# Banded attention in a decoder layer: where the value blocks are fetched, when the scores start, and when the first expert tile comes

## The chip, the cores and the metric

One core of one Trainium2 chip. The metric is the device time of one execution in microseconds (us); lower is better. All data are float32.

## The reference

A decoder layer with normalisation after each part, on 8 batches of 512 rows of 256 channels. There are three parts, and each adds its output to its input and normalises the rows:

```python
x = layernorm(x + banded_attention(x))        # 16 heads of 16 channels, window of 17 rows
x = layernorm(x + cross_attention(x, ctx))    # causal, one head of 256 channels, keys = values = ctx
x = layernorm(x + experts(x))                 # top 2 of 8 experts, 256 -> 1024 -> 256, gelu
```

The first part has a soft window, whose width and sharpness come out of each row:

```python
q = ln(silu(x @ Wq)); k, v = split(silu(x @ Wkv)); k = ln(k)      # ln by head
wp = silu(x @ Wwin + bwin)
width, sharp = sigmoid(wp[..., :16]) * 8 + 0.5, sigmoid(wp[..., 16:]) * 9.5 + 0.5
scores[l, h, w] = sum_d q[l, h, d] * k[l + w - 8, h, d] / 4        # w = 0..16
mask = sigmoid((width - abs(w - 8)) * sharp)
attn = softmax(scores - (1 - mask) * 10000)
out = silu((sum_w attn[w] * v[l + w - 8]) @ Wout)
```

The third part picks two experts a row by `x @ router_w.T`, weighs them by a softmax over the two, and adds `gelu(x @ w1[e].T) @ w2[e].T` of each.

## The kernel before

Five engines run instruction streams of their own: PE (matrix products and transposes), DVE (vector work), ACT (activations and copies), POOL (here nearly all DMA issues, the indirect ones among them) and SP (DMA issues alone). A scheduler decides the order on all but SP; SP's stream has the order in which the kernel's text is traced. `issue_after(ins)` puts the next instruction behind `ins` on the same engine.

The work is a software pipeline over rounds b = -2 to 8. A round lets several streams run side by side: cross-attention and routing of batch b (`crossed`), the weighted sums of banded attention of batch b+1 (`attended`), projections and scores of batch b+2 (`scores`), loads (`fetched`), and the expert tiles that can be run by then (`experts`). `together` (L1114) takes steps from the streams by their shares of the round: each stream has an amount of work, a start and an end in the round, and the stream with the least progress steps next. That sets the order in which the text is traced, SP's order, and the scheduler's preference.

Banded attention of a batch:

- `scores` projects the rows (L321, L322), normalises q and k, transposes them (L367), and multiplies q against k for half of the heads at a time (c = 0, 1) into `row`, which ACT's queue stores to a scratch in DRAM (`band`). `read_scores(c)` (L384) reads the band back in the layout of the softmax, `s`, by a DMA on POOL. `ws` (L395, POOL) carries what the mask is made of, `pen`. The values are stored to `vband`, and for batches 0 to 2 (`BANDED` = 3) two blocks of them, `vblock`, 320 KB each, are read back at L443 by POOL. In this kernel that happens a round before they are used, between and after the two score reads.
- `summed` (L497, batches 0 to 2) takes the softmax of each half on DVE and ACT, beginning with L519 (`s` and `pen`) and ending with L534 (times 1/sum). SP stores the weights to DRAM, `aband` (L541; c = 0 in four pieces, c = 1 in one), and fetches them back in blocks of 128 rows, `arow`, 160 KB each as two DMAs (`fetch`, L503, L507), of which two fit. There are eight blocks (two halves by four groups g0 to g3). PE transposes each (`paT`, L579), DVE and ACT copy the result (`aT`, L583), and PE multiplies it with `vblock` (`pw`, L557). Batches 3 to 7 go through `weighted`, which has neither.
- `attended` multiplies the sums with Wout (`py`, L599), ACT applies silu into `y` (L607, one buffer), DVE adds it to the rows (L609, twice a batch), and `layernorm` follows: statistics and `off` (L292) on DVE, the rows themselves on ACT (L295).

Cross-attention transposes the context and the rows (L248), multiplies (L715) and takes its softmax (with the transposes `pt` of L704 behind it). `route` picks the experts, copies a token's number into the rows (L811, an entry of the list `urgent`), and scatters the rows to the experts' regions in DRAM, `sorted_x` (L819, POOL); `plan` (L834) lays out the tiles that are ready, and its last DVE instruction (L903) is an entry of `urgent` too.

An expert tile is loaded by `load_tile` on SP (L937): two numbers read from memory (L940, L941), two halves of w1 (L961) and of w2 (L967), 512 KB each, and the rows `xs` (L946). The first tile of a round waits for the scatters before it, and has its `xs` behind the weights. `turned` transposes `xs` on PE (`pxs`, L1001). Round b = 1 has the first tile of all, one.

Of the kernel before, what the change touches and what calls it, by code (L numbers as in the profile page):

```python
# [10 lines left out]
ALU = mybir.AluOpType  # L11
# [4 lines left out]
L = 512  # L16
# [6 lines left out]
C = HH * D  # L23
QB = P // 2
SPAN = QB + W - 1
# [19 lines left out]
def decoder_layer_kernel(  # L45
# [16 lines left out]
    nc = tc.nc  # L62
    B = x.shape[0]
# [105 lines left out]
    def blank_rows(at):  # L169
# [2 lines left out]
            sorted_x[bass.ds(at, TS), :].rearrange("(p f) c -> p (f c)", p=P), blank  # L172
        )

    scattered, adds, out_of, read, turns, urgent = [], [], {}, [], [], []

    vband = [
        [dpool.tile([L + 2 * HALO, C], F32, name=f"vband{u}{c}") for c in range(2)]  # L180
        for u in range(2)
    ]
# [122 lines left out]
    def scores(b, xb):  # L305
# [129 lines left out]
        vh = []  # L435
        if b < BANDED:
            vb = apool.tile([P, 2, L // QB, C], F32, tag="vh", name="vblock", bufs=2)
        for c in range(2):
            src = vband[b % 2][c][:, :]
            if b < BANDED:  # L440

                with tc.issue_after(read[-1].ins):
                    nc.gpsimd.dma_start(  # L443
                        vb[0:SPAN, c],
                        bass.AP(
                            tensor=src.tensor,
                            offset=src.offset,
                            ap=[[C, SPAN], [QB * C, L // QB], [1, C]],
                        ),
                    )  # L450
                vh.append(vb[:, c])
                yield 0.3
                if c == 0:
                    read_scores(1)
                continue
            vhc = apool.tile([P, T + 2 * HALO, C], F32, tag="vh", name="vhalo", bufs=2)
            with tc.issue_after(read[-1].ins):
                nc.gpsimd.dma_start(
                    vhc.rearrange("p t c -> p (t c)"),
                    bass.AP(  # L460
                        tensor=src.tensor,
                        offset=src.offset,
                        ap=[[T * C, P], [1, (T + 2 * HALO) * C]],
                    ),
                )
            vh.append(vhc)
            yield 0.3
            if c == 0:
                read_scores(1)
# [27 lines left out]
    def summed(b):  # L497


        groups = [(c, g) for c in range(2) for g in range(T)]  # L500
        rows_of = {}

        def fetch(c, g):  # L503
            ar = apool.tile([P, HG, SPAN, 2], F32, tag="a", name="arow", bufs=2)
            for u in range(2):
                ub = (g * P + u * QB) * (LINE + 2)
                nc.sync.dma_start(  # L507
                    ar[u * QB : (u + 1) * QB].rearrange("p r k u -> p (r k u)"),
                    aband[c][ub : ub + QB * LINE].rearrange("(p n) -> p n", p=QB),
                )  # L510
            rows_of[c, g] = ar

        s, pen, vh = out_of.pop(b)
        for c in range(2):
            sc = s[c]


            with tc.issue_after(urgent[-1].ins) if urgent and c == 0 else nullcontext():
                nc.vector.scalar_tensor_tensor(  # L519
                    sc, pen[:, c], -4.0e4, sc, ALU.mult, ALU.add  # L520
                )
            flat = sc.rearrange("p t r w u -> p (t r) w u")
            byw = sc.rearrange("p t r w u -> p (t r) u w")
            full = [P, T * HG, W, 2]
            top = spool.tile([P, T * HG, 2], F32, tag="top", name="top")
            nc.vector.tensor_reduce(top, byw, AX.X, ALU.max)
            nc.vector.tensor_tensor(
                flat, flat, top[:, :, None, :].to_broadcast(full), ALU.subtract
            )
            nc.scalar.activation(sc, sc, AF.Exp, scale=0.25)  # L530
            den = spool.tile([P, T * HG, 2], F32, tag="den", name="den")
            nc.vector.tensor_reduce(den, byw, AX.X, ALU.add)
            nc.vector.reciprocal(den, den)
            nc.vector.tensor_tensor(  # L534
                flat, flat, den[:, :, None, :].to_broadcast(full), ALU.mult
            )
            lines = aband[c].rearrange("(p t n) -> p t n", p=P, t=T)[:, :, 0:LINE]

            parts = T if c == 0 else 1
            for ps in (slice(k * P // parts, (k + 1) * P // parts) for k in range(parts)):  # L540
                nc.sync.dma_start(  # L541
                    lines[ps].rearrange("p t (r n) -> p t r n", r=HG)[:, :, :, 0 : 2 * W],
                    sc[ps].rearrange("p t r w u -> p t r (w u)"),
                )
            if c == 0:

                for early in groups[:2]:
                    fetch(*early)
            yield 5.0
        oT = apool.tile([P, KC, L], F32, tag="T", name="oT", bufs=4)  # L550
        aT = apool.tile([P, 2, HG, 2, P], F32, tag="prod", name="aT")

        def sums(c, g):
            po = ps_o.tile([P, 2, 2, QB], F32, tag="o", name="pw")
            for u in range(2):
                for r in range(HG):
                    nc.tensor.matmul(  # L557
                        po[32 * r : 32 * r + 32, u],
                        vh[c][0:SPAN, 2 * g + u, 32 * r : 32 * r + 32],
                        aT[0:SPAN, g % 2, r, :, u * QB : (u + 1) * QB],  # L560
                        start=True,
                        stop=True,
                    )

            to = oT[:, c, g * P : (g + 1) * P].rearrange("c (u q) -> c u q", u=2)
            nc.scalar.mul(to, po[:, :, 0, :], par[:, 0:1])
            nc.vector.scalar_tensor_tensor(
                to, po[:, :, 1, :], par[:, 1:2], to, ALU.mult, ALU.add
            )

        for k, (c, g) in enumerate(groups):
            if 2 <= k + 1 < len(groups):
                fetch(*groups[k + 1])
            ar = rows_of.pop((c, g))
            for i in range(2):
                pt = ps_h.tile([P, 2, 2, P], F32, tag="h", name="paT")
                for r in range(2):
                    for u in range(2):
                        nc.tensor.transpose(  # L579
                            pt[0:SPAN, r, u, :], ar[:, 2 * i + r, :, u], ident  # L580
                        )
                put = nc.scalar.copy if i else nc.vector.tensor_copy
                put(aT[0:SPAN, g % 2, 2 * i : 2 * i + 2], pt[0:SPAN])  # L583
            if k:
                sums(*groups[k - 1])
            yield 1.4
        sums(*groups[-1])
        yield 0.8
        return oT

    def attended(b, xb):

        oT = yield from (summed if b < BANDED else weighted)(b)
        for jj in range(T // 2):
            py = ps_m.tile([P, 2, E], F32, tag="m", name="py")
            for j in range(2):
                for kc in range(KC):
                    at = (2 * jj + j) * P
                    nc.tensor.matmul(  # L599
                        py[:, j, :],  # L600
                        oT[:, kc, at : at + P],
                        wout_sb[:, kc, :],
                        start=(kc == 0),
                        stop=(kc == KC - 1),
                    )
            y = spool.tile([P, 2, E], F32, tag="y", name="y", bufs=1)
            nc.scalar.activation(y, py, AF.Silu)  # L607
            xj = xb[:, 2 * jj : 2 * jj + 2, :]
            nc.vector.tensor_tensor(xj, xj, y, ALU.add)  # L609
            yield 2.4  # L610
        layernorm(xb)
        yield 2.6
# [522 lines left out]
    had = 0  # L1135
    for b in range(-2, B + 1):
        streams = [(fetched(b), 1.0, 0.45, 1.0)] if b > -2 else []
        if 0 <= b < B:
            streams.append((crossed(b), 31.0, 0.0, 0.93))
        if 0 <= b + 1 < B:  # L1140
            streams.append((attended(b + 1, rows[b + 1][:, :, 0:E]), 29.4 if b + 1 < BANDED else 60.0, 0.08, 1.0))
        if b + 2 < B:
            streams.append((scores(b + 2, rows[b + 2][:, :, 0:E]), 38.0, 0.0, 0.88))
        m = max(0, -((NX * (TS - 1) - 2 * L * b) // TS)) if b < B else tiles_max
        if m > had:
            streams.append((experts(m - had, b == B), (m - had) * 7.2, 0.0, 1.0))
            had = m
        together(*streams)

# [56 lines left out]
```

## Time and profile before

| | |
| --- | --- |
| time, median of 3 runs | 1030.87 us (1028.61 to 1030.87) |
| profiled execution, its own time | 1036.22 us |
| its span (first to last instruction) | 1034.5 us |
| mean granted PE clock | 0.929 |
| PE, DVE, ACT, POOL busy | 903.6, 639.8, 549.1, 253.6 us |
| DMA moved | 252.09 MB, mean 244 GB/s |
| `vblock` fetches | 6 on POOL, 1.08 us each to issue, 5.3 to 7.7 us to landing |
| `arow` fetches on SP | 48 DMAs of two halves, 160.0 KB each |

A page describes one execution. Busy times count instructions that work, not the issue of DMAs, branches or waits. A line of the waits names an engine and a line of the kernel, what it waited for, the us in all, how often, and the longest. A line of the timeline has the start in us, the duration, the engine (a `q` behind it: its DMA issues), line, operation, tiles as out<-in, and in brackets the idle time before it and what ended that.

### The profile page before, as it was taken

How to read it: one execution, taken by the hardware profiler on the slowest of the kernel's cores; microseconds unless marked ns; L12 is line 12 of the kernel's file. 1: busy time of each engine (PE TensorE's matmuls, PEld its weight loads, DVE VectorE, ACT ScalarE, POOL GpSimd, SP SyncE). 2: the span in 40 equal slices, each digit the busy share in tenths (PEclk: the TensorE clock that was granted, in tenths of full speed). 3: DMA queues.
4: the chain of work that ended last, by engine and by line, in shares of the span. 5: the costliest groups of instructions: out<-in, count | busy, mean ns of one | idle time of the engine just before them, and what ended most of it. 6: DMA issues, size and time to landing. Idle time of an engine off the chain costs nothing. (4 is left out here: it accounts for less than half of the span.)

```text
span 1034.5 us, 18962 instructions
## 1 busy us (share of the span) xinstructions
PE 903.6 (87%) x6336; PEld 753.2 (73%) x6336; DVE 639.8 (62%) x2130; ACT 549.1 (53%) x955; POOL 253.6 (25%) x211
## 2 busy tenths in 40 slices
PE   5758888679989899999999989999999988999970
PEld 3435565457678778787788678888998988999960
DVE  5375773773689879979994989399943331111106
ACT  4465655567556647677755775476365311222224
POOL 1101000400411241125222522252341241121221
PEclk9588897889889899999999999899999999999995
DMA  8585654673798879588879897998898899999949
GB/s 207 145 139 142 128 129 113 194 160 89 254 343 252 250 273 298 174 263 308 264 218 273 293 282 195 273 343 290 258 282 256 274 266 379 319 331 318 335 114 323
DMA packets 129267, 252.09 MB, mean 244 GB/s; under 512 B 29680, under 2 KB 76848, under 8 KB 127888
## 3 DMA queue, kind: packets, MB, share of 16 engines
q1 hardware_dynamic: 89456, 183.30, 55.2%
q0 software_dynamic: 17824, 41.86, 16.4%
q10 hardware_dynamic: 21888, 25.70, 9.3%
q8 instruction: 52, 0.85, 0.3%
q14 instruction: 47, 0.39, 0.1%
HBM read 193.44 MB, written 57.36 MB: 242 GB/s over the span
## 5 line engine op out<-in xcount | busy, mean ns | idle before, releaser
L1015 PEld LDWEIGHTS ph<-xsT,w1h 128*128 128x128 f32 x2176 | 263.8, 195 | 14.0 <-DVE xsT L1004 4.9
L1015 PE MATMUL ph<-xsT,w1h 128*128 128x128 f32 x2176 | 270.5, 280 | 3.1 <-DVE xsT L1004 3.0
L1032 PE MATMUL pf<-w2h,h 128*128 128x256 f32 x1088 | 256.7, 387 | 3.3 <-ACT h L1023 3.3
L1032 PEld LDWEIGHTS pf<-w2h,h 128*128 128x128 f32 x1088 | 204.3, 194 | 32.6 <-ACT h L1023 5.7
L1041 POOL DMA_INDIRECT total<-ye,toi x68 | 122.3, 1798 | 420.5 <-ACT ye L1040 121.7
L1023 ACT ACTIVATE h<-ph 128x512 f32<-128x512 f32 x136 | 81.2, 598 | 121.7 <-PE ph L1015 116.7
L1004 DVE COPY xsT<-pxs 128x256 f32<-128x256 f32 x68 | 28.5, 419 | 175.2 <-PE pxs L1001 175.2
L655 DVE TENSOR_TENSOR prod<-prod 128x1024 f32<-128x1024 f32 (+3 forms) x160 | 103.3, 645 | 0.3
L1040 ACT ACTIVATE ye<-pf,g 128x256 f32<-128x256 f32 x68 | 32.2, 473 | 125.0 <-PE pf L1032 115.5
L647 DVE TENSOR_TENSOR prod<-vhalo,a 128x2176 f32<-128x2176 f32 x40 | 96.4, 2410 | 0.2
L819 POOL DMA_INDIRECT sorted_x<-xr,to x64 | 78.4, 1225 | 23.4 <-issue 16.4
L413 PE MATMUL pq<-kT,qT 32*64 32x160 f32 x1024 | 60.1, 389 | 17.5 <-DVE row L422 9.4
L387 POOL DMA_DIRECT2D s<-band x16 | 24.3, 1520 | 205.6 <-DMA band<-row 98.3
L321 PE MATMUL pa<-wall,xT 128*128 128x512 f32 x128 | 69.3, 629 | 5.5 <-ACT qk L323 2.8
L413 PEld LDWEIGHTS pq<-kT,qT 32*64 32x64 f32 x1024 | 36.0, 156 | 33.3 <-DVE row L422 11.9
L1023 ACT ACT_TABLE_LOAD x39 | 50.0, 1283 | 7.2 <-PE ph L1015 5.7
L422 ACT COPY row<-pq 128x320 f32<-128x320 f32 x104 | 37.9, 433 | 29.8 <-PE pq L413 24.7
L322 PEld LDWEIGHTS pb<-wall,xT 128*128 128x128 f32 x128 | 24.9, 197 | 35.8 <-issue 24.7
L579 PE MATMUL paT<-ident,arow 128*80 128x128 f32 x192 | 32.0, 309 | 18.3 <-DMA arow<-aband 14.0
L322 PE MATMUL pb<-wall,xT 128*128 128x288 f32 x128 | 42.4, 419 | 4.1 <-DVE wp L325 2.5
L689 PE MATMUL po<-c,prT 128*128 128x256 f32 x160 | 40.9, 386 | 4.3 <-ACT prT L708 4.2
L295 ACT ACTIVATE xr<-xr,off,rs 128x256 f32<-128x256 f32 x64 | 33.2, 592 | 21.2 <-DVE off L292 21.1
(196 smaller groups left out, 1376.7 us busy)
## 6 DMA issues: line engine op xcount, KB each, us to landing
w1h<-in_w_dram SPq DMA_DIRECT2D x136, 512.0 KB
w2h<-in_w_dram SPq DMA_DIRECT2D x136, 512.0 KB
band<-row ACTq DMA_DIRECT2D x64, 320.0 KB
vhalo<-vband POOLq DMA_DIRECT2D x10, 1280.0 KB, 9.6
xs<-sorted_x SPq DMA_DIRECT2D x68, 132.5 KB
arow<-aband SPq DMA_DIRECT2D x48, 160.0 KB
s<-band POOLq DMA_DIRECT2D x16, 272.0 KB, 6.3
xr<-in_x_dram SPq DMA_DIRECT2D x8, 512.0 KB
```

The costliest lines, as they stand in the source:

```text
L321: nc.tensor.matmul(pa, lhs, wall[:, kc, 0 : 2 * E], **se)
L322: turns.append(nc.tensor.matmul(pb, lhs, wall[:, kc, 2 * E :], **se))
L413: nc.tensor.matmul(pq[r][u * QB : (u + 1) * QB, ii], qT[rs, c, at : at + QB], kT[rs, c, :, at : at + SPAN].rearrange("p u k -> p k u"), st ...
L422: put(row[:, :, r], pq[r])
L647: nc.vector.tensor_tensor(prod.rearrange("p w (h d) -> p w h d", d=D), vh[c][:, t : t + W, :].rearrange("p w (h d) -> p w h d", d=D), a[:, ...
L655: nc.vector.tensor_tensor(prod[:, 0:n, :], prod[:, 0:n, :], prod[:, n : 2 * n, :], ALU.add)
L689: nc.tensor.matmul(po, probsT[j][:, i * P : (i + 1) * P], c[:, i, :], start=(i == 0), stop=(i == j),)
L819: sent = nc.gpsimd.indirect_dma_start(out=sorted_x[:, :], out_offset=bass.IndirectOffsetOnAxis(ap=to[:, n, j : j + 1], axis=0), in_=xr[:, ...
L1015: nc.tensor.matmul(ph[:, u, :], w1s[hf][:, kc, f * P : (f + 1) * P], xT[:, kc, :], start=(kc == 0), stop=(kc == KC - 1),)
L1023: nc.scalar.activation(h, ph, AF.Gelu)
L1032: nc.tensor.matmul(po, hs[fc // HU][:, fc % HU, j * P : (j + 1) * P], w2s[hf][:, f, :], start=(fc == 0), stop=(fc == NF - 1),)
L1041: add = nc.gpsimd.indirect_dma_start(out=total[:, :], out_offset=bass.IndirectOffsetOnAxis(ap=toi[:, j : j + 1], axis=0), in_=y, in_offset ...
```

## The change

There are three edits. The `vblock` fetches leave `scores` and POOL; SP issues them in `summed`, for each half after the store of that half's weights, and ahead of the fetches of `arow` that come next. The list `added` keeps the additions of `y` to the rows, and the first instruction of the c = 0 softmax of a batch is put behind the last entry of `urgent`, or, while that is empty, of `added`. When it is traced for batch 1, `urgent` is empty. The stream of experts starts at 0.45 of its round, not at 0, where no tile has been run before, which is in round b = 1 alone.

By the text and the streams, SP's order in round 1 goes from `where`, w1, w2, `xs`, then stores and fetches of batch 2's weights, to: stores of c = 0, `vblock`, fetches of g0 and g1, store of c = 1, `vblock`, fetch of g2, loads of x and of the context, `where`, w1, w2, `xs`, fetch of g3 and the others.

```diff
-    scattered, adds, out_of, read, turns, urgent = [], [], {}, [], [], []
+    scattered, adds, out_of, read, turns, urgent, added = [], [], {}, [], [], [], []
...
             if b < BANDED:
 
-                with tc.issue_after(read[-1].ins):
-                    nc.gpsimd.dma_start(
-                        vb[0:SPAN, c],
-                        bass.AP(
-                            tensor=src.tensor,
-                            offset=src.offset,
-                            ap=[[C, SPAN], [QB * C, L // QB], [1, C]],
-                        ),
-                    )
                 vh.append(vb[:, c])
                 yield 0.3
                 if c == 0:
...
-            with tc.issue_after(urgent[-1].ins) if urgent and c == 0 else nullcontext():
+            first = (urgent or added)[-1:] if c == 0 else []
+            with tc.issue_after(first[0].ins) if first else nullcontext():
                 nc.vector.scalar_tensor_tensor(
                     sc, pen[:, c], -4.0e4, sc, ALU.mult, ALU.add
                 )
...
                     sc[ps].rearrange("p t r w u -> p t r (w u)"),
                 )
+
+            src = vband[b % 2][c][:, :]
+            nc.sync.dma_start(
+                vh[c][0:SPAN],
+                bass.AP(
+                    tensor=src.tensor,
+                    offset=src.offset,
+                    ap=[[C, SPAN], [QB * C, L // QB], [1, C]],
+                ),
+            )
             if c == 0:
 
                 for early in groups[:2]:
...
-            nc.vector.tensor_tensor(xj, xj, y, ALU.add)
+            added.append(nc.vector.tensor_tensor(xj, xj, y, ALU.add))
...
-            streams.append((experts(m - had, b == B), (m - had) * 7.2, 0.0, 1.0))
+
+            begin = 0.0 if had else 0.45
+            streams.append((experts(m - had, b == B), (m - had) * 7.2, begin, 1.0))
             had = m
```

## Prediction

> **What bounds the kernel now.** I read the page first, for the busy shares and the 40 slices. The page's first part has PE at 87% of the span with no other engine near it. The second part shows where PE isn't full: up to the tenth slice (25.9 us each, so up to about 260 us), at the ninth, and at the end.
>
> ```profile
> span 1034.5 us, 18962 instructions
> PE 903.6 (87%) x6336; PEld 753.2 (73%) x6336; DVE 639.8 (62%) x2130; ACT 549.1 (53%) x955; POOL 253.6 (25%) x211
> PE   5758888679989899999999989999999988999970
> ```
>
> Then the window table, cut at the rounds that the diff touches (round A: batch 0's weighted sums; B: batch 1's; C: batch 2's, halved at 208), and the rest. Columns: window, its length, busy us of PE, PEld, DVE, ACT and POOL, granted PE clock, DMA share, GB/s.
>
> ```profile
> 44.00:103.00 59.00, 41.91 (x410) 28.10 (x409) 33.48 (x66) 33.10 (x59) 6.98 (x7) 0.79 0.70 149
> 103.00:178.00 75.00, 61.96 (x478) 42.70 (x476) 48.03 (x141) 46.69 (x88) 5.33 (x6) 0.86 0.57 121
> 178.00:208.00 30.00, 20.26 (x69) 13.26 (x69) 19.64 (x86) 15.60 (x26) 11.53 (x11) 0.84 0.64 194
> 208.00:266.00 58.00, 51.72 (x456) 38.73 (x457) 30.55 (x100) 38.84 (x76) 2.58 (x3) 0.85 0.60 151
> 266.00:1034.00 768.00, 702.41 (x4776) 614.17 (x4774) 487.71 (x1694) 394.38 (x673) 223.55 (x161) 0.96 0.88 276
> ```
>
> PE is idle 17.1, 13.0, 9.7 and 6.3 us in the first four windows: 46 us is all that this change can work on. In the compiled program the order of every engine's instructions is the old one from about 260 us on, and PE is busy there for 702 of 768 us, so I carry a shift at 266 us through to the end unchanged. Last, the waits of PE (window 44 to 300 us) and of SP's queue (40 to 300; columns: us in all, times, longest), and the places on the timeline (start, us, what; in brackets the idle time before it and what ended that).
>
> ```profile
> PE paT L579 <- DMA arow<-aband: 14.0, 4, 6.4
> PE pxs L1001 <- DMA xs<-sorted_x: 10.4, 2, 7.1
> PE pt L704 <- ACT pr L728: 2.8, 2, 2.5
> SPq L946 <- DMA sorted_x<-xr,to: 17.6, 3, 10.0
> SPq L507 <- DMA aband<-s: 8.2, 5, 5.1
> ```
>
> ```profile
> 68.27 1.91 PE L579 MATMUL paT<-ident,arow 128*80 128x128 f32 x8 [6.40 <-DMA arow<-aband]
> 111.43 0.66 PE L248 MATMUL pt<-ident,c 128*128 128x128 f32 x4 [2.73 <-ACT y L607]
> 115.56 0.16 DVE L292 SCALAR_TENSOR_TENSOR off<-mv,rs 128x4 f32<-128x4 f32 x1
> 117.23 0.73 DVE L519 SCALAR_TENSOR_TENSOR s<-pen,s 128x544 f32<-128x544 f32 x1 [0.50 <-DMA s<-band]
> 207.97 0.69 PE L1001 MATMUL pxs<-ident,xs 128*128 128x128 f32 x2 [7.09 <-DMA xs<-sorted_x]
> 208.45 1.91 PE L248 MATMUL pt<-ident,xr 128*128 128x128 f32 x8
> ```
>
> Each edit aims at one of these waits: 6.40 in A, 2.73 in B, 7.09 in C.
>
> **Edit 1, the six value fetches, POOL to SP (mostly A).** POOL loses 6 issues of 1.08 us (the rows of L443 on POOL), 6.5 us in all, on an engine that is 25% busy: worth nothing by itself. SP gains 6 issues; the nearest row, the load of x on SP (L91), has 0.59 us, so 3.5 us, all behind a store that SP had been waiting to issue.
>
> The gain: two stretches of DMA. The c=0 block is issued at 47.21, beside the c=0 score read (45.99) that DVE waits for; the c=1 block at 55.77, beside the c=1 score read (272 KB, 6.4 us to landing) and the four c=0 weight stores. There the DMA view of 56 to 64 us shows POOL's queue (the block and the read) taking as much of the engines' time as SP's and ACT's transfers together:
>
> ```profile
> q0 software_dynamic: 192, 0.61, 39.8%
> q1 hardware_dynamic: 2098, 0.28, 39.6%
> vblock<-vband POOLq DMA_DIRECT2D x1, 320.0 KB, 7.7
> ```
>
> SP waits 5.1 us for the stores before it can fetch rows, and PE 6.40 for those rows. Without the blocks the c=0 scores may land up to 2.4 sooner (the blocks' own landings spread from 5.3 to 7.7), and the stores in half of the 5.1, 2.5 sooner. Against that the block stands ahead of the rows on SP: 0.6 of issue, and 320 KB at about 200 GB/s, 1.6; between 0.6 and 2.2, and I take 1, since the rows' own 3.8 us from issue to landing (64.43 to 68.27) runs beside part of it. So 2.4 + 2.5 − 1 = 4 for the first transposes, out of the 6.40. For c=1 the same 1 is paid ahead of group 2, where PE waited 3.56 us at 78.49 already, and the new order puts the copy for that group behind `width` (83.32, behind a load of `ws`). **A −3**, ends −6 (nearly the whole wait) and +2 (no gain, and the block paid whole).
>
> The Trainium skill's page "DMA: Bandwidth & Descriptors", section "Issuing engines are not separate DMA queues", speaks against this edit: transfers from any engine run on the same 16 DMA engines, and another issuer saves only issue time. By that rule A would be 0 and the whole sum −1.5; the rule doesn't deny that the order changes, which is what I count.
>
> **Edit 2, batch 1's first score instruction behind batch 0's last row sum (B), batch 2's behind route's copy (C).** In B the row sum (L609) stood behind three score instructions on DVE (107.85 to 110.1), and ACT's second `y`, which has one buffer, behind that. The wait of 2.73 on PE goes. What is late next: in the new order the c=1 score instruction, which waits for its read (0.50 us before 117.23 in the trace, so landing at 116.7), stands with its maximum and the c=0 sums ahead of `off`. `off` goes from 115.56 to about 118 (116.7 plus 0.73 plus about one 0.7), 2.4 later, 3.2 if two more are ahead. ACT normalises the rows from there (2.08 us) and only then drains the first tile's values. PE, 2.7 us early, has filled its four PSUM buffers (two tiles) by 117 and stops until ACT is through, 118.2 + 2.1 + 0.6 + a table load of 1.28 = 122.2. It took up that place (the second half of tile 2) at 120.76. That is +1.4, and the c=0 weights come about as late, with the rows that hang on them: **B +2**, ends −1 (ACT drains sooner) and +3.1 (the 3.2 whole).
>
> **Edit 3, the first expert tile from 0.45 of its round (C).** Removed: PE's 7.09 at the `xs` transposes, and SP's 10.0 at L946, which kept the c=0 weights, finished at 195.9, from being stored until 206.31. The x transposes behind (208.45) may go when the projections are done (200.87) and their buffers drained, about 1.5 us more: 202.4, so −6.0. What is late next: the softmax of cross-attention, which had its other work before it and now has less; the trace's own wait of that kind is 2.5 us (L704), and I give one back. The scores behind the route's copy start 4 us later than in the trace (191.8 for 187.6), but are stored at once, at about 200, still before 206: no cost. **C −3.5**, ends −7 and 0.
>
> Added there: the first tile's 2 MB of weights and xs, behind the loads of x and c (1 MB), all ahead of the rows of group 3 on SP. 3.15 MB from 214.5 us (x's load stood at 219.49, and comes some 5 sooner when the stores before it wait no more) at about 300 GB/s (the trace moved the 2 MB from 192.7 in 9.5 us, 220 with other traffic, and x and c alone at 380) takes 10.5 us: 225. A row fetch needs 3.8 more: 229. PE came to group 3 at 229.9 in the trace, at about 227 to 231 after the shifts. So it is hidden, by some 2 us or less, and is no term in my sum; without that cover it is the third rival.
>
> **Sum.** −3 + 2 − 3.5 = −4.5. The profiled execution took 1036.22 us (span 1034.5 and 1.7 outside), so 1031.7; that execution is 5.35 above the median of the runs, so the median becomes 1026.4. About 0.3% (3.1 us) is what can be told from no change.
>
> **Rivals.** (1) *The gains come whole*: A −6, C −7, B 0, so −13: 1018. For it: three waits removed are 16 us together. Against it: the buffers and softmax waits named above. (2) *The idle time only moves*: −1, +2, −1, so 0: 1030.9. For it: PE is short of input in A and B for many small reasons, no one of them over 6.4 us. Against it: the 7.09 stands alone before work that is ready. (3) *The weights hold up the rows*: place, SP's queue ahead of group 3 of batch 2; price, 3.15 MB at the 194 GB/s of the window from 178 to 208 takes 16.2 us, so the rows land at 214.5 + 16.2 + 3.8 = 234.5, while PE, 6 us early, is there at about 225: a wait of 9.5. It decides once the wait passes the 6 us gained. Then −1 + 2 − 6 + 9.5 = +4.5: 1035.4, and +8 if A ends on its loss. Against it: SP may issue the weights before 214.5.
>
> **How the numbers follow.** Forecast 0.36 (its own range, with two ends never met together, 1022 to 1030), gains whole 0.15, no net change 0.19, weights ahead 0.30. Faster by over 0.3%: most of the first (0.30), all of the second and 0.03 of the third, 0.48. Within: 0.05, 0.12 and 0.02, 0.19. Slower: 0.33. The range runs from 1016 (rival 1 with a little more) to 1039 (rival 3 with A's loss).
>
> **What would show it.** In the changed profile PE's wait at the first row transposes of round A is 2 to 3 us rather than 6.40; the wait on `y` near 110 us is gone while `off` is nearer to 118; the `xs` transposes come after the q and k transposes of round C with a wait under 1 us; PE's wait at group 3 near 228 us is under 2 us; and the work that stood at 266 us stands at 261 to 262. A wait of over 5 us for rows or xs between 222 and 236 would be rival 3; a shift at 266 us that grows later would make the whole method wrong.

## The result and the profile after

The changed kernel takes 1047.29 us (median of 6 runs, 1036.13 to 1048.75) against 1029.74 for the kernel before (6 runs, 1027.03 to 1033.87): ratio 1.0138, 95% interval 1.0102 to 1.0174, so 10 to 18 us slower. The forecast was 1026.4, with a range to 1039. The profiled execution took 1046.66 us, 10.4 more than that of before. On the page:

```profile
span 1045.0 us, 18958 instructions
PE 913.6 (87%) x6336; PEld 754.5 (72%) x6336; DVE 638.3 (61%) x2130; ACT 549.6 (53%) x954; POOL 246.5 (24%) x205
PE   5767869758989899999999999997999989999970
```

The shares hardly move, but the microseconds do: PE is busy 10.0 us longer than before, with as many instructions, and idle only 0.5 us longer (131.4 for 130.9). So what the edits took out of PE's waits came back as other waits, and the rest of the loss is work that took longer; the mean granted PE clock is 0.921 for 0.929. The window table shows where:

```profile
44.00:103.00 59.00, 46.75 (x376) 28.54 (x376) 32.13 (x63) 31.34 (x55) 3.47 (x3) 0.77 0.62 137
103.00:178.00 75.00, 58.35 (x410) 39.62 (x412) 45.17 (x124) 46.56 (x85) 3.51 (x3) 0.84 0.52 115
178.00:208.00 30.00, 24.31 (x140) 15.70 (x136) 22.81 (x104) 17.27 (x29) 11.44 (x10) 0.89 0.43 107
208.00:266.00 58.00, 42.85 (x364) 30.30 (x364) 26.90 (x81) 32.78 (x67) 2.05 (x3) 0.82 0.69 165
```

Round B has 410 PE instructions where the kernel before had 478, and the second half of C 364 for 456: the windows cut at fixed times, so the counts show by how much the work has slipped. Landmarks of the two traces show the slip growing: ACT's first `y` of batch 0 at 106.81 for 105.70, of batch 1 at 188.29 for 181.79, of batch 2 at 279.27 for 268.10. After 300 us it is between 7 and 8 us up to 480. Most of the loss is made in B and C. Some of it is made in A, which the trace of before hides, since it is late there itself: its first `y` is at 105.70, and at 100.64 to 103.48 in the three runs below without edit 1.

Most of what the prediction wanted to see of its three edits is there, and that makes the case instructive. PE's first wait for rows is 3.15 us, not 6.40. The wait of 2.73 for batch 0's `y` is gone (of batch 1's there is one of 0.36). `off` is at 118.74 (predicted: about 118). The `xs` transposes stand after the q and k transposes with no wait to speak of. Two signs are not there: PE's wait for rows near 228 us is 3.84, not under 2, and the work that stood at 266 us has moved back, not forward. Here are those places, PE and DVE on the timeline of the changed kernel (its lines are 3 to 9 off those of before: L582 is `paT`, L248 the context's transposes):

```profile
65.03 1.94 PE L582 MATMUL paT<-ident,arow 128*80 128x128 f32 x8 [3.15 <-DMA arow<-aband]
192.10 0.66 PE L248 MATMUL pt<-ident,c 128*128 128x128 f32 x4 [0.36 <-ACT y L610]
118.74 0.15 DVE L292 SCALAR_TENSOR_TENSOR off<-mv,rs 128x4 f32<-128x4 f32 x1
244.38 0.38 PE L1004 MATMUL pxs<-ident,xs 128*128 128x128 f32 x2
```

What is new stands on another engine. DVE's wait at `width` (us in all, times, longest), window 44 to 300, of the changed kernel:

```profile
DVE width L466 <- DMA ws<-wband: 20.8, 3, 9.0
```

For the kernel before, the wait of `width` is 1.5 us in two times, in B and in C:

```profile
141.27 0.20 DVE L475 TENSOR_SCALAR width<-ws 128x64 f32<-128x64 f32 x1 [1.00 <-DMA ws<-wband]
223.20 0.19 DVE L475 TENSOR_SCALAR width<-ws 128x64 f32<-128x64 f32 x1 [0.47 <-DMA ws<-wband]
```

On the changed kernel's DVE timeline the three stalls are these, and below them what waits behind the second and the third on PE:

```profile
78.78 0.19 DVE L466 TENSOR_SCALAR width<-ws 128x64 f32<-128x64 f32 x1 [3.64 <-DMA ws<-wband]
145.95 0.19 DVE L466 TENSOR_SCALAR width<-ws 128x64 f32<-128x64 f32 x1 [8.13 <-DMA ws<-wband]
229.68 0.19 DVE L466 TENSOR_SCALAR width<-ws 128x64 f32<-128x64 f32 x1 [8.98 <-DMA ws<-wband]
...
147.82 0.90 PE L707 MATMUL pt<-ident,pr 128*128 128x128 f32 x3 [4.30 <-ACT pr L731]
232.44 1.08 PE L582 MATMUL paT<-ident,arow 128*80 128x128 f32 x4 [4.20 <-DVE aT L586]
```

How to read them: DVE runs its stream in order, and at 137.8 us it comes to `width`, an instruction whose result is wanted only in the next round. Its input, 64 KB of `ws`, is not there until 145.95. Behind it stand `xtop` (the softmax of cross-attention, which ACT and then PE wait for: the 4.30), the normalising of q and k, and the copy `aT`, which PE waits for (the 4.20 in C). DVE is 61% busy, and still its place in line costs PE.

Whether that is the cause, and which edit brought it, is what the runs below tell. Their times are also given as ratios to the kernel before as it ran beside them, since its own median was 1030.4, 1033.9 and 1028.4 us beside the three groups.

### The profile page after: what moved, and what is told of

Read it like the earlier page. It is cut to its first block, busy times and chain, and to the rows that moved or that the text cites. A ratio compares the mean times of both kernels' runs of the same rounds, so it can differ in the third digit from the quotient of the medians.

```text
span 1045.0 us, 18958 instructions
## 1 busy us (share of the span) xinstructions
PE 913.6 (87%) x6336; PEld 754.5 (72%) x6336; DVE 638.3 (61%) x2130; ACT 549.6 (53%) x954; POOL 246.5 (24%) x205
## 5 line engine op out<-in xcount | busy, mean ns | idle before, releaser
L1035 PE MATMUL pf<-w2h,h 128*128 128x256 f32 x1088 | 259.3, 389 | 3.4 <-ACT h L1026 3.4
L582 PE MATMUL paT<-ident,arow 128*80 128x128 f32 x192 | 34.2, 322 | 19.3 <-DMA arow<-aband 10.9
L718 PE MATMUL ps<-cT,x1T 128*128 128x128 f32 (+3 forms) x128 | 47.4, 488 | 0.3 <-ACT x1T L257 0.2
L582 PEld LDWEIGHTS paT<-ident,arow 128*80 128x80 f32 x192 | 24.5, 163 | 29.5 <-issue 13.8
```

The lines of the kernel that those rows point to most:

```text
L582: nc.tensor.transpose(pt[0:SPAN, r, u, :], ar[:, 2 * i + r, :, u], ident)
L718: nc.tensor.matmul(ps[:, :n], xT[:, kc, j * P : n], cT[:, kc, :n], start=(kc == 0), stop=(kc == KC - 1),)
L1035: nc.tensor.matmul(po, hs[fc // HU][:, fc % HU, j * P : (j + 1) * P], w2s[hf][:, f, :], start=(fc == 0), stop=(fc == NF - 1),)
```

## Which edit: each one alone

**Edit 1 alone** (the hunks on the six value fetches, nothing else).

> Only edit 1: the six value blocks go from POOL to SP; the scores' place and the start of the first expert tile are as before. Theory F (the fetches cost it: their new place makes the scheduler order round A to C anew, and the blocks stand ahead of the rows on SP): 8 to 12 us over before, the second y of round 0 already level or later, and most of the loss in rounds B and C. Theory S (the scores behind the row sums cost it): within 2 us of before. Theory T (the late first tile costs it): within 2 us of before, and the 7 us wait for xs in round C still there.

Measured: 1048.87 us, ratio 1.0188 (1.0130 to 1.0246), about 19 us slower. Theory F holds, though its 8 to 12 us were too few; the whole loss is here. Its DVE and PE waits, and the third stall:

```profile
DVE width L466 <- DMA ws<-wband: 16.4, 3, 6.4
...
PE pw L558 <- DVE aT L584: 9.4, 2, 6.2
PE paT L580 <- DVE aT L584: 7.4, 5, 5.9
...
234.16 0.20 DVE L466 TENSOR_SCALAR width<-ws 128x64 f32<-128x64 f32 x1 [6.39 <-DMA ws<-wband]
```

PE waits 16.8 us behind DVE's copies where in the kernel before it waits 5.5 (3.0 and 2.5).

These waits are not the whole of it. From 44 us to ACT's fifth gelu (304.84 us in before, 321.25 in only_fetch) PE is idle for 57.8 us where it was 51.4, and busy for 219.5 where it was 209.4: of the 16.4 us, some 10 are work that takes longer. The granted clock there is 0.82 for 0.85, and over the runs its mean is 0.918 for 0.928 of the kernel before beside them. What the clock does to PE's work can be read in the trace of before: the eight transposes of the rows take 1.97 us where the granted clock is 0.50, and 1.04 where it is 1.00:

```profile
46.14 1.97 PE L248 MATMUL pt<-ident,xr 128*128 128x128 f32 x8 [0.63 <-DVE row L422]
107.67 1.04 PE L248 MATMUL pt<-ident,xr 128*128 128x128 f32 x8
```

No run tests what lowers the clock. It is no chance of a chip or an hour, for it follows the kernel: in the second group it is 0.931 in the run that holds `width` back, 0.916 in fetch_behind_rows, which doesn't, and 0.927 in the kernel before.

**Edit 2 alone.**

```diff
-            with tc.issue_after(urgent[-1].ins) if urgent and c == 0 else nullcontext():
+            first = (urgent or added)[-1:] if c == 0 else []
+            with tc.issue_after(first[0].ins) if first else nullcontext():
```

> Only edit 2: the first score instruction behind the last row sum or route's copy. SP's and POOL's orders are as before. Theory F: within 2 us of before. Theory S: 4 to 7 us over before, with off of batch 0 about 3 us later, and waits of PE on cross-attention's softmax in round B (4.3 and 1.9 us in the whole change) that before doesn't have. Theory T: within 2 us of before.

Measured: 1029.14 us, ratio 1.0000 (0.9966 to 1.0034). Theory S falls. PE's wait on `y` in B is gone, and PE stops for 4.35 us instead at the projections (119.10 us), behind DVE's `wp` (L325); the two cancel within 3.5 us.

**Edit 3 alone.**

```diff
+            begin = 0.0 if had else 0.45
-            streams.append((experts(m - had, b == B), (m - had) * 7.2, 0.0, 1.0))
+            streams.append((experts(m - had, b == B), (m - had) * 7.2, begin, 1.0))
```

> Only edit 3: the first expert tile starts at 0.45 of its round. Rounds A and B are as before, instruction by instruction. Theory F and theory S: 2 to 5 us under before, since PE's 7.09 us wait goes and at most half is given back. Theory T: 3 to 6 us over before, with PE waiting 4 us or more for the rows of group 2 or 3 behind the weights in round C.

Measured: 1025.19 us, ratio 0.9963 (0.9932 to 0.9995), 3.8 us faster. Theory T falls. No wait for rows between 200 and 240 us is over 1.5 us in its trace, so the 2 MB ahead of group 3 on SP are hidden.

**Edits 2 and 3 without edit 1.**

> Edits 2 and 3 without edit 1: the value blocks stay on POOL. Theory F: 1 to 5 us under before. Theory S: 1 to 5 us over before (the loss in B less the gain in C). Theory T: 3 us or more over before. If edit 1 only costs together with another, this is fast and so is only_fetch.

Measured: 1026.22 us, ratio 0.9977 (0.9940 to 1.0015). So the parts are +1.9%, 0.0% and −0.4%; their sum of +1.5% lies in the interval of the whole change.

## Which part of edit 1: DVE's order or SP's queue

In the compiled program, edit 1 moves `width` on DVE. This counts how many of the copies `aT` and of the softmax's masked scores (`causal`) of its round stand ahead of it, for rounds A, B and C:

```
kernel              copies A, B, C    causal B, C
before              3, 2, 2           3, 3
only_fetch          2, 2, 0           2, 2
whole change        2, 2, 1           3, 2
only_scores         3, 2, 2           3, 3
only_tile           3, 2, 3           3, 4
```

In A and C copies that PE waits for are now behind `width`. In B what moved is small: the normalising of q and k and the later copies are behind it in each of these kernels, and in only_fetch so is one more step of the softmax. In the whole change its place in B is the old one by these counts, yet DVE came to it 2.4 us sooner than in the trace of before (137.8 for 140.3: there, DVE had waited 4.12 us for PE's scores just ahead of it) and `ws` was asked for 2.7 us later (139.37 for 136.63) and took 1.9 us longer to land (6.6 for 4.6). The three make up the 7.1 us between the stalls of 8.13 and 1.00. So the counts tell of a risk; the stall itself is the difference of two times.

**`width` put back behind the fourth copy of its round, edit 1 otherwise whole.** `copies` collects DVE's copies of the current `summed` and is emptied at its start:

```diff
-            nc.vector.tensor_scalar(
+            behind_copy = copies[3 : 3 + 1] if b <= BANDED else []
+            with tc.issue_after(behind_copy[0].ins) if behind_copy else nullcontext():
+                nc.vector.tensor_scalar(
...
-                put(aT[0:SPAN, g % 2, 2 * i : 2 * i + 2], pt[0:SPAN])
+                copied = put(aT[0:SPAN, g % 2, 2 * i : 2 * i + 2], pt[0:SPAN])
+                if not i:
+                    copies.append(copied)
```

> Edit 1 alone, and DVE's `width` instruction of batches 1 to 3 put behind the fourth copy aT of its round. SP's and POOL's orders are those of only_fetch. Theory W (edit 1 makes the scheduler put `width`, which waits for the load of ws, ahead of the copies that PE needs, and DVE stands 4.4, 5.6 and 6.4 us there): the three stalls and PE's waits of 3.3, 6.2 and 5.9 us behind them go, and the time falls by 12 to 18 us from only_fetch, to 1031 to 1037 or below. Theory Q (the blocks on SP's queue ahead of the rows, or their packets, cost it): 1043 or more, since SP and the packets are as they were.

Measured: 1029.55 us, ratio 0.9953 (0.9922 to 0.9983). The loss is gone, and more. `width` has no idle time ahead of it in any of the three rounds, and PE's waits on `aT` are down to 1.4 us in all:

```profile
81.53 0.18 DVE L468 TENSOR_SCALAR width<-ws 128x64 f32<-128x64 f32 x1
146.97 0.17 DVE L468 TENSOR_SCALAR width<-ws 128x64 f32<-128x64 f32 x1
229.91 0.18 DVE L468 TENSOR_SCALAR width<-ws 128x64 f32<-128x64 f32 x1
...
PE pw L561 <- DVE aT L587: 0.9, 2, 0.6
PE paT L583 <- DVE aT L587: 0.5, 1, 0.5
```

SP's and POOL's streams are those of only_fetch, instruction by instruction. Theory Q, at 1043 or more, does not hold. Two more runs move the blocks themselves:

**The blocks behind the first row fetches.**

```diff
             if c == 0:
                 for early in groups[:2]:
                     fetch(*early)
+            src = vband[b % 2][c][:, :]
+            nc.sync.dma_start(vh[c][0:SPAN], ...)
```

> Edit 1 alone, but the blocks are issued on SP behind the first row fetches of c = 0 (and behind the store of c = 1 as before, which has none). In its compiled order `width` stands ahead of the third copy in round A and in round B as in only_fetch, but behind two copies in round C, as in the kernel before. Theory W: the stalls of A and B stay and that of C goes: 5 to 8 us under only_fetch, about 1041 to 1044. Theory Q: nearly all of it goes for c = 0, 1030 to 1036.

Measured: 1050.57 us, ratio 1.0144 (1.0099 to 1.0190): 4 to 5 us under only_fetch by the ratios, with intervals that overlap, and nowhere near theory Q's 1030 to 1036. Its DVE waits have the two stalls that theory W left to it, of 7.0 and 7.1 us, both longer than in only_fetch (4.4 and 5.6); W's 5 to 8 us were reckoned without that:

```profile
DVE width L466 <- DMA ws<-wband: 14.1, 2, 7.1
```

**The blocks at the new place, but by POOL** (`nc.gpsimd.dma_start` for `nc.sync.dma_start`).

> The blocks are fetched at edit 1's place in the text, but by POOL, not SP. Here the scheduler puts `width` where the kernel before has it in rounds A and B, and behind four copies in C. Theory W: 1026 to 1034, with DVE's stalls on ws under 2 us. Theory Q as far as it is SP's queue: 1028 to 1034 as well; as far as it is the blocks in flight beside the rows: 1040 or more. It says whether SP itself is needed for the loss.

Measured: 1038.83 us, ratio 1.0045 (1.0013 to 1.0077): 4.6 us slower than before, above theory W's 1026 to 1034 and under the 1040 for blocks in flight. Three quarters of the loss are gone. Both the place of `width` and SP's queue are here nearly those of before, so this run alone doesn't part them. A stall of 4.3 us is left in B. POOL's timeline says where from; its stream is in order too, and `ws` is behind the two blocks:

```profile
137.55 1.46 POOL L538 DMA_DIRECT2D vblock<-vband  x2 [23.00 <-DMA vband<-v]
139.00 0.57 POOL L395 DMA_DIRECT2D ws<-wband  x1
```

**The whole change with `width` late.**

> The whole change, and `width` of batches 1 to 3 behind the fourth copy of its round. Theory W: the gains of edits 2 and 3 (no_fetch 1026) show without the stalls: 1020 to 1030, 17 to 27 us under the whole change. Theory Q: within 5 us of the whole change's 1047.

Measured: 1030.39 us, ratio 0.9966 (0.9935 to 0.9997), where the whole change has 1.0138. One ordering edge on DVE is worth 1.7%.

## The controls, and a better version

A pin may be a gain by itself, so the same edge went into the kernel before.

> The kernel before with nothing but `width` of batches 1 to 3 behind the fourth copy of its round: the control for fetch_width_late. The kernel before stands only 1.5 us at `width`, so if the pin only takes the stalls away, it is worth 0 to 3 us here: ratio 0.997 to 1.002. If the pin is a gain of its own (a better order for other reasons), the ratio is 0.985 or so, and fetch_width_late at 0.9953 would still hide a loss of edit 1 of some 10 us.

Measured: 1023.07 us, ratio 0.9954 (0.9926 to 0.9981). So it is a gain, of 4.7 us where I had allowed 0 to 3: the stalls of 1.5 us are not all that the later place gives. What the rest is I didn't find. The comparison it was made for is plain: with `width` held, the kernel with edit 1 has 0.9953 and without it 0.9954. Edit 1 itself costs nothing and gives nothing here, to within some 4 us.

The second pair takes the wait away: batches 1 to 3 leave out their load of `ws` and use that of batch 0.

> Edit 1 alone, and batches 1 to 3 use the ws of batch 0: their loads of ws are left out (their mask is then that of other rows), so that `width` has nothing to wait for, though its place in DVE's order is ahead of all or all but one of the copies. Theory W: the time is that of before_ws_kept within 4 us, near 1030. If an early place of `width` costs by displacing work rather than by its wait, or if edit 1 costs in some other way, it stays 8 us or more above before_ws_kept.

> The kernel before with the same loads of ws left out (batches 1 to 3 use batch 0's): the control for fetch_ws_kept. Both theories: 1025 to 1032, at most 4 us under the kernel before, which waits only 1.5 us for ws.

Measured: 1033.31 us, ratio 1.0048 (1.0012 to 1.0085), against 1032.69, ratio 1.0046 (1.0010 to 1.0082). `width` stands ahead of nearly all copies in both. With nothing to wait for, the scheduler has put these instructions between 32 and 72 us, ahead of rounds B and C, so the pair takes away the early place in these rounds along with the wait. Again the two are level: edit 1 costs nothing where DVE doesn't stand at `width`. Both are 0.5% above the kernel before, which neither theory had expected. The scheduler puts the work on `pen` among the softmax of the scores here, and the granted clock of the two is lower (means 0.926 and 0.924, for 0.930 of before beside them); which of the two it is was not tested.

The last run was for a version better than both kernels.

> Edits 2 and 3 without edit 1, and `width` behind the fourth copy: the best that the runs so far point to. no_fetch still stands 2.7 us at `width`, once; theory W: no_fetch's ratio 0.9977 or up to 3 us less, 0.993 to 0.998. If edit 1 has a gain of its own that the stalls hid, this is slower than all_width_late (0.9966).

Measured: 1027.92 us, ratio 1.0006 (0.9972 to 1.0040). That missed: edits 2 and 3 and the late `width` don't add. Its trace has PE waiting 6.3 us, 5.6 of it at once, for DVE's `wp` (L325), where before has 2.5; but no_fetch has 6.0 and 5.0 there, so that is edit 2's wait and doesn't explain the miss. Its granted clock is 0.925 in the mean, for 0.930 of before beside it. Why is open.

This run is also a third pair, with all_width_late, and by its own expectation it speaks for a gain of edit 1: without edit 1 the ratio is 1.0006, with it 0.9966. That is 4 us, with intervals that overlap, and the two other pairs show none. An effect of edit 1 itself of 3 us or so is neither shown nor excluded.

The best of all is the kernel before with the edge alone (0.9954), level with fetch_width_late.

## Why the prediction was wrong

**Step that failed: edit 1, term A, −3 us.** The words "the new order also puts the copy for that group behind `width`" were there, and "behind a load of `ws`". But the 1 us that was taken off the gain beside them is the price of the block on SP; `width` never got one, and was never looked for in B and C. The sum had no term for an instruction of another kind that moves past the engine's other work. In its place the runs showed stalls of 4.4, 5.6 and 6.4 us (only_fetch) and 3.6, 8.1 and 9.0 (whole change), with PE behind them. A second thing was put at nothing: "46 us is all that this change can work on" counts PE's idle time alone, and 10 of the 16.4 us by which only_fetch was late at 305 us are PE busy longer, at a lower granted clock.

The price could be read from the trace of before. `ws` landed there at 141.27 in B and 223.20 in C; DVE waited for it at both places, if only 1.0 and 0.5 us, so nothing earlier could have had it. In the new order `width` comes after `st` of B, which ended at 135.76, and ahead of the first copy of C, which began at 217.56. The differences are 5.5 and 5.6 us; the runs gave 5.6 and 6.4 in only_fetch. The short waits of 1.0 and 0.5 were the warning: the instruction was already as early as its data. For A there was no such warning. DVE didn't wait at `width` there (83.32, with `ws` landed at about 81.5); in only_fetch it came to it at 73.4, 9.9 us sooner, and `ws` landed at 77.8, only 3.7 sooner.

**The gain in A.** The c = 1 scores do come sooner with edit 1: their first instruction on DVE (L519 in before) is at 56.1 to 56.2 us in only_fetch and the whole change, and at 57.8 to 58.9 in the three runs without it. But the first row transposes start at 64.8 and 65.0 there and at 65.2 to 65.5 in those three. That they start at 68.27 in the kernel before is mostly that one execution, which was already 2 us late at its first scores (51.34, for 49.0 to 49.6). So the 4 us that I took out of the 6.40 wait were nearly all not to be had. With `width` held late, the first `y` of batch 0 is at 103.03 and 103.65 us with edit 1 and at 104.80 and 102.20 without it: no gain in A. In the times, two of the three pairs with edit 1 as the only difference leave nothing of −3. This is what the Trainium skill's page "DMA: Bandwidth & Descriptors", section "Issuing engines are not separate DMA queues", would make of it (another issuer saves only issue time; A would be 0); an effect of 3 us is not excluded by the pairs.

**Edit 2, term B, +2 us.** Its size is 0.0 ± 3.5 us when alone, inside its bounds. The wait on `y` goes and PE stops at the projections, as argued. That `off` came to 118.74 as forecast is luck: only_fetch, without edit 2, has it at 118.36, and with edit 2 but not edit 1 it is at 116.00 (only_scores) and 113.23 (no_fetch).

**Edit 3, term C, −3.5 us.** Measured −3.8 alone. The 7.09 us wait goes and part of it comes back at the next stops, as argued (in only_tile 2.29 at the x transposes, 1.41 for rows at 205.9 and 1.41 at a softmax at 222.5). B and C together, −1.5 by the sum, are −2.4 (−6.2 to +1.5) in no_fetch.

**Rivals.** None was right. The third had the right sign and the wrong place: rows of batch 2 are waited for 3.84 us in the changed kernel, not 9.5, and the weights ahead of them on SP cost nothing alone. Nor is it a sign of them that `ws` takes 8.2 us to land in C, for 6.6 at most in only_fetch: it takes 8.2 there in fetch_behind_rows too, which issues the weights some 23 us ahead of it.

**The method.** "The order is the old one from about 260 us on" held, and with it the shift stayed 7 to 8 us up to 480 us; later it went between 1 and 11, with 10.5 at the end, so a shift is carried through only roughly. But the order was read the wrong way round: all the differences lay ahead of 260 us, in a listing where each move of an instruction that waits for a DMA should have been priced, and I priced only those that the diff names.

## What to carry to other kernels

Where a scheduler orders the engines, compare the compiled orders before and after, and for each instruction that reads a freshly loaded tile ask two times: when does its data land by the trace, and when does the engine reach its new place. The difference is a stall of everything behind it, also on an engine that is 61% busy. A short wait already at that instruction says that it has no slack to give; none, as in A, doesn't say that it has. If its result isn't needed soon, try an explicit edge behind the work that others wait for: here it was worth 1.7% in the changed kernel, and 0.46% in the one before, no less than the best of the three edits (0.37%, with intervals that overlap). And read the granted clock beside the idle time: of this loss, idle time is the smaller part in the traces.

## What the runs showed of the hardware

The same blocks travel in other packets when SP issues them. The page's queues, kernel before and then the changed one (packets, MB, share of 16 engines):

```profile
q1 hardware_dynamic: 89456, 183.30, 55.2%
q0 software_dynamic: 17824, 41.86, 16.4%
```

```profile
q1 hardware_dynamic: 93392, 185.27, 55.2%
q0 software_dynamic: 17248, 39.89, 15.5%
```

1.97 MB left POOL's queue as 576 packets, 3.4 KB each, and came to SP's as 3936 of 500 bytes. fetch_late_pool, with the blocks at the new place but issued by POOL, has the packets of before, so it is the issuer that decides. I hadn't expected it, and as the two level pairs show, it cost nothing that these runs can tell.
